# Constant products first on TensorE, the input check split, last outputs in two passes and a new order for the first four graphs, in a two-layer graph transformer

## The chip, the cores and the metric

The kernel runs on one core of a Trainium2 chip. The metric is the device time of one execution in microseconds (us), the median of several runs. A core has engines that run side by side, each with its own queue of instructions that it works off in order: PE (TensorE, matrix products; PEld is the loading of their weights), DVE (VectorE), ACT (ScalarE), POOL (GpSimd) and SP (SyncE, which only issues transfers here). Engines wait for one another through semaphores.

## The reference, cut to what matters

64 graphs of 256 nodes with 256 features, all float32, go through two attention layers of 8 heads of 32. Layer 0 weighs values by the relation that stands in `adj` (0 or 1 in these inputs) and has a feed-forward part of 1024; layer 1 masks by `adj` and normalises a joined product.

```python
# layer 0
q, k = heads(src @ Wq + bq), heads(src @ Wk + bk)
attn = softmax(q @ k.T / sqrt(32))
out = sum((attn * (adj == r)) @ heads(src @ Wv[r] + bv[r]) for r in range(4))
x = ln(src + out @ Wo + bo, g1, beta1)
x = ln(x + gelu(x @ W1 + b1) @ W2 + b2, g2, beta2)
# layer 1
e = heads(x @ Wq) @ heads(x @ Wk).T
e = where(e >= 0, e, 0.2 * e)
h = softmax(where(adj > 0, e, -9e15)) @ heads(x @ Wv)
out = ln(h, g1, b1)
out = ln(concatenate([out, x]) @ Wffn.T, g2, b2) + x
```

## The kernel before, in words

One graph is one program of some 140 steps (`program`, in `fast_path`). A step is an emit function with an engine and the tiles that it reads and writes; a helper like `linear_T`, `score`, `stats` or `normalise` appends it, so many rows of the profile bear the line of a helper. A graph's names end in digits: `q0` and `k0` are the transposed queries and keys of layer 0, `q1` and `k1` those of layer 1.

The steps of all 64 graphs are merged into one list by `in_order` (line 46): each step has a key, `g * PERIOD` plus an offset, and the list is sorted by it. For the middle graphs the offset comes from `STARTS`, for the first four from `FIRST`, for the last three from `LAST`; keys are no times, only the order counts. Every engine gets its own steps in the order of the list. At the ends (`at_end`: the first two graphs, the last three) a matrix is transposed by products with `ident` on PE (line 413); in between it goes through DRAM (lines 387 to 400).

Per graph on PE: `pq0`, `pk0` (line 351), `pva0` and `pva1` (values, line 668, which need `wv0` with the difference of its two relations, line 600 on DVE), two groups of scores `s` (line 487), weighted sums `po` (lines 526 and 533), `pwo`, the feed-forward products `ph` and `pw2` (lines 716 and 734), then layer 1. Around them ACT takes exponentials (line 503) and adds biases from `cols` (line 375; its first such step also loads a table), DVE adds the mask to scores (line 512), takes reciprocals (line 542) and statistics (lines 453 to 457), and POOL makes `neg` from `adj` (line 646), adds pairs (line 559) and raises variances to -0.5 (`rs`, line 462, 128x2).

All loads are issued by SP: those of the weights by `fetch` (line 571), those of a graph by `load` (line 342). Their order at the start is `xT`, `cols`, `wk0`, `wq0`, `x`, `wf`, `wv0` (two), `rows` (the first three), `adj`, `wk1`, `wq1`, `wo`, the next `xT`, `w2`, the rest of `rows`, `w1`. Eight transfers can be out: a later one waits for the landing of the one eight places ahead.

Some constants are prepared on the way, by steps of graph 0: `bf` is a product of `wide` and `wf` (line 613, copied at 618), `wf` is scaled by a gain (line 620), and `pmean` (line 624) is a product of `mean_w` with it, which line 630 subtracts. Lines 604 and 605 add shifts in `rows`.

The fast path holds for inputs within limits. Every graph leaves 13 `flags` per partition: sums of exponentials from ACT (line 503), a count of `adj` (`junk`, line 650) and minima of `po` from DVE (line 550). At the end of the program lines 823 to 830 compare all 64 x 13 of them, take the minimum into `held`, add that up over the partitions by a product (`pheld`, line 829) and turn it into an integer, `bad`. Every engine loads `bad` into a register (line 1106) and branches over a general path that isn't run with these inputs (line 1107).

A graph's output is `(pwa - mean) * rs3 * g21 + x2`: `normalise` (line 468), a product with the row `g21` (line 479), a sum (line 811), and a store by SP (line 815). The last two graphs (`alone`) do all three on DVE, the others the last two on POOL.

Of the kernel before, what the change touches and what calls it, by code (L numbers as in the profile page):

```python
# [20 lines left out]
LIMIT = 1.0e30  # L21
# [13 lines left out]
class Op:  # L35


    __slots__ = ("eng", "name", "emit", "reads", "writes", "tiles", "g")

    def __init__(self, eng, name, emit, reads, writes, g):  # L40
        self.eng, self.name, self.emit, self.g = eng, name, emit, g
        self.reads, self.writes = reads, writes
        self.tiles = {k.partition("/")[0] for k in (*reads, *writes) if not k.startswith("c_")}


def in_order(programs, starts, period, first, last):
# [4 lines left out]
    for g, p in enumerate(programs):  # L51
# [75 lines left out]
        -10256.79, -10417.946, -10418.845, -9655.276, -9647.458, -9418.15, -8780.756, -8806.383, -9016.741, -9513.158,  # L127
        -9495.078, -8590.155, -10003.295, -9291.904, -8309.175, -9386.676, -9231.17, -8787.021, -8660.76, -8501.398,
        -10584.811, -10218.322, -9608.334, -9104.436, -8066.002, -8804.961, -9825.295, -9578.272, -9914.488, -9442.87,
        -8813.641, -8607.962, -8849.406, -8632.071, -8937.919, -8812.934, -8791.331, -8734.75, -8483.473, -8864.473,  # L130
        -8822.078, -8429.134, -8776.728, -8405.192, -7953.761, -7894.531, -8299.242, -8717.176, -8646.31, -8662.099,
        -8343.426, -8329.008, -8597.096, -8514.051, -8426.417, -8189.977, -7960.378, -7718.59, -7712.398, -7156.11,
        -7563.49, -7208.499, -7179.238, -6917.369, -6917.367, -6842.704, -6710.303, -6711.003, -5706.559, -6495.228,
        -6280.588, -5865.4, -5592.334, -6199.311, -5863.221, -6468.444, -6370.931, -4538.172, -4524.407, -4477.482,
        -4262.426, -3973.372, -3910.404, -3900.969, -3877.771, -3834.718, -3824.557, -3691.587, -3679.897, -3639.541,
        -3597.827, -3679.895, -3670.439, -3501.055, -3451.404, -3588.256, -3531.636, -2474.703, -2461.465, -2676.921,
        -2656.758, -3125.063, -3042.896, -2882.815, -2732.056, -2363.914, -1353.064, -2880.589, -2907.254, -2822.537,
        -2673.746, -2335.009, -1303.618, -1270.494, -1110.428, -1102.74, -2879.234, -2657.203, -2352.556, -2279.244,
        -2160.732, -1901.876, -2634.306, -2653.396, -2012.309, -2009.408, -1888.68, -1502.012, -1412.116, -1401.834,
        -1416.364, -1030.225, -1028.517, -845.649, -962.518, -780.505, -766.279, -749.221, -709.195, -670.931,  # L140
        -611.671, -592.943,
    ],
    [
        -9082.793, -8821.413, -8584.273, -7679.799, -6811.314, -7104.159, -8654.94, -8159.713, -8706.211, -7742.971,
        -7680.585, -6931.674, -7419.902, -7096.988, -7703.279, -7671.026, -7657.377, -6498.021, -7183.946, -7456.855,
        -7450.09, -7209.053, -7018.734, -5702.193, -5336.158, -5268.731, -5511.652, -7298.293, -6672.664, -6484.273,
        -6263.457, -6347.867, -6896.885, -6809.914, -6006.901, -5819.284, -5608.438, -5269.483, -4803.162, -5294.853,
        -4599.474, -4599.472, -4523.688, -4264.846, -4180.662, -4093.925, -3856.605, -3530.581, -2717.744, -3767.55,
        -3761.457, -3803.533, -3754.922, -3678.334, -3632.2, -3255.184, -2820.341, -2245.675, -2226.134, -2052.422,
        -2039.8, -1660.362, -1625.035, -1571.564, -1553.578, -1513.777, -1477.183, -1431.984, -1430.337, -1422.225,  # L150
        -1283.864, -806.335, -713.143, -1134.104, -964.675, -1040.209, -962.322, -637.997, -270.909, -429.146,
        -415.015, -902.241, -790.878, -678.22, -644.005, -304.133, -210.429, -750.975, -854.699, -673.468, -515.045,
        -207.195, 203.932, 204.235, 208.581, 204.66, -655.094, -463.233, -624.339, -356.78, -220.376, 151.773,
        -324.271, -584.5, -91.29, 187.862, 205.121, 208.965, 211.757, 217.346, 216.045, 221.82, 233.633, 247.638,
        251.141, 252.624, 253.253, 254.651, 255.687, 261.447, 266.334, 284.16,
    ],
    [
        -4966.772, -5312.443, -5889.946, -5039.664, -5159.898, -4403.862, -4858.218, -4629.529, -4776.965, -4743.102,
        -3624.438, -3257.491, -3668.955, -3429.095, -4199.202, -3902.433, -4134.244, -3680.958, -3569.518, -4163.448,
        -3791.904, -3660.555, -3903.418, -3088.911, -2951.813, -2855.197, -2965.02, -3779.594, -3631.033, -3662.701,  # L160
        -3261.638, -3534.707, -3599.126, -3348.893, -3327.559, -3335.702, -3058.321, -2879.469, -2723.157, -2940.722,
        -2500.765, -2419.982, -2276.826, -2220.814, -2013.151, -1889.428, -1759.468, -1742.956, -1603.331, -1264.512,
        -1189.663, -1485.202, -1299.287, -1432.334, -1367.98, -1493.639, -1413.183, -1010.364, -835.846, -342.676,
        -201.659, -201.446, -56.663, 32.587, 88.02, 119.909, 119.911, 119.913, 128.596, 142.281, 150.543, 153.74,
        168.786, 168.788, 169.449, 224.646, 270.798, 169.527, 175.654, 169.451, 170.984, 176.522, 181.529, 216.866,
        216.884, 176.871, 180.112, 181.424, 192.101, 195.643, 195.645, 177.642, 178.723, 179.252, 183.741, 199.835,
        208.317, 210.029, 210.062, 209.5, 181.49, 189.03, 182.007, 192.546, 208.878, 210.609, 189.653, 192.363,
        200.391, 206.241, 210.864, 218.9, 223.499, 223.501, 220.829, 224.953, 229.115, 229.117, 239.344, 239.346,
        237.172, 242.289, 242.553, 242.555, 246.814, 255.425, 276.721, 301.931,
    ],  # L170
    [
        -2616.915, -3738.122, -3620.23, -2516.76, -1581.888, -1074.953, -2411.766, -2359.837, -2551.424, -1876.812,
        -1291.539, -1214.653, -2577.138, -2502.882, -1561.046, -1537.605, -1435.037, -1321.017, -1285.438, -1542.519,
        -1499.312, -1171.673, -1282.107, -975.95, -721.667, -614.834, -791.494, -1342.782, -1251.881, -1324.781,
        -1047.049, -1006.905, -1196.205, -1109.182, -970.883, -1012.21, -901.837, -576.093, -575.311, -594.413,
        -511.897, -399.597, -363.529, -361.357, -259.089, -121.886, 103.011, 105.823, 105.825, 129.412, 150.16,
        113.575, 113.766, 138.118, 144.328, 134.023, 139.222, 135.909, 142.051, 154.14, 154.142, 155.882, 156.568,
        157.309, 157.311, 157.661, 157.915, 158.185, 158.711, 159.186, 159.188, 160.249, 160.251, 160.956, 167.451,
        210.29, 232.587, 171.569, 175.025, 170.655, 175.703, 199.606, 201.092, 184.548, 190.236, 177.141, 177.143,
        178.154, 178.156, 184.769, 199.293, 178.1, 178.056, 178.58, 195.805, 196.124, 204.141, 205.044, 205.046,  # L180
        205.281, 183.277, 193.889, 188.544, 197.528, 200.755, 203.056, 190.546, 183.279, 190.548, 190.55, 204.236,
        208.318, 210.997, 213.457, 212.603, 216.36, 216.673, 219.934, 223.927, 223.929, 220.362, 224.498, 225.099,
        229.925, 229.927, 233.872, 233.874, 233.876,
# [39 lines left out]
        9503.563, 10042.577, 10382.53, 9566.925, 10478.524, 10510.355, 10670.284, 10757.907, 10767.9, 11156.775,  # L223
        11402.842,
# [12 lines left out]
        16007.55, 16095.484, 16016.502, 16372.924, 17323.706, 17389.259, 17464.619, 17489.423, 17525.145, 17585.795,  # L237
# [4 lines left out]
def fast_path(nc, tc, a, out, bad):  # L242
# [13 lines left out]
    with ExitStack() as ctx:  # L256
# [64 lines left out]
        def program(g):  # L321
# [7 lines left out]
            def op(eng, reads, writes, emit):  # L329


                for w in writes:
                    name, _, tag = w.partition(":")
                    tags.setdefault(name, tag or name)
                writes = [w.partition(":")[0] for w in writes]
                name = writes[0] if writes else f"{eng}:{reads[0]}"
                used[name] = used.get(name, 0) + 1
                o = Op(eng, f"{name}#{used[name]}" if used[name] > 1 else name, emit, reads, writes, g)
                ops.append(o)
# [225 lines left out]

            if g == 0:

                def fetch(name, *pairs):
                    def emit():
                        for t, ap in pairs:  # L570
                            nc.sync.dma_start(out=t, in_=ap)
# [566 lines left out]
```

## Time and profile before

| what | us |
|---|---|
| median of 3 runs (2815.0 to 2818.29) | 2815.79 |
| the profiled execution | 2813.84 |
| its span, first to last instruction | 2812.1 |
| PE busy | 2779.5 |
| DVE, POOL, ACT busy | 2071.8, 1988.2, 1939.3 |
| mean granted TensorE clock | 0.998 of full |

In the profile a row of the timeline has its start and its length in us, engine, line, operation, the tile written and those read, shapes, and in brackets how long the engine was idle before it and what ended that. A product of float32 shows as two records. The table of stages has, for each stretch, its length, then for each engine its busy time and number of instructions (PE, PEld, DVE, ACT, POOL), the granted TensorE clock, the share of the transfer engines and GB/s. Rows with q behind the engine's name are its queue: issues, register loads, branches and waits; there the columns are the number, then least, median and greatest length in ns, then first and last start. Lines of the profile are those of the kernel before, unless said otherwise.

### The profile page before, as it was taken

To read this page: it belongs to the slowest core of one execution; us is meant where nothing else is said; L and a number is where in the kernel's file an instruction comes from. 1 tells how busy PE (TensorE), PEld (TensorE's weight loads), DVE (VectorE), ACT (ScalarE), POOL (GpSimd) and SP (SyncE) were. 2 spreads that over 40 slices of the span, in tenths; PEclk is the share of its full clock that TensorE was granted. 3 is DMA by queue.
4 is the path that set the end of the run, shared out by engine and by line. 5 is a ranking of instruction groups with operands and counts; after the bars stand their busy time and mean duration, and the time that the engine had idled before them with its cause. 6 is when DMAs were issued, how large, how long until landed. Compare 5 with 4: busy or idle time off the path is not lost.

```text
span 2812.1 us, 54239 instructions
## 1 busy us (share of the span) xinstructions
PE 2779.5 (99%) x21094; PEld 2085.7 (74%) x21094; DVE 2071.8 (74%) x3853; ACT 1939.3 (69%) x3131; POOL 1988.2 (71%) x1526
## 2 busy tenths in 40 slices
PE   8999999999999999999999999999999999999996
PEld 6777777777777777777777777777777777777774
DVE  5667777777777777777777777777777777777776
ACT  5766767767767667677676676776766767767663
POOL 3668677677676676776766867768667677677773
PEclk9999999999999999999999999999999999999999
DMA  3012122222222222222222222222222122231100
GB/s 132 24 46 71 52 75 61 54 72 57 61 65 58 68 61 54 73 59 58 69 61 61 62 52 76 57 57 69 60 61 64 51 74 60 54 83 49 50 27 13
DMA packets 269750, 169.55 MB, mean 60 GB/s; under 512 B 18608, under 2 KB 268976, under 8 KB 269488
## 3 DMA queue, kind: packets, MB, share of 16 engines
q1 hardware_dynamic: 269488, 166.02, 22.2%
q8 instruction: 169, 2.77, 0.4%
q14 instruction: 93, 0.76, 0.1%
HBM read 102.77 MB, written 63.18 MB: 59 GB/s over the span
## 4 chain that ended last, share of the span: by engine, by line
PE 93%; DVE 3%; POOL 1%; ACT 1%; DMA 1%; issue 1%; SPq 0%; DVEq 0%; POOLq 0%; ACTq 0%
PE pw L734 15%; PE ph L716 15%; PE po L526 12%; PE s L487 9%; PE pk L351 8%; PE pva L668 8%; PE pq L351 7%; PE pv L365 4%; PE pwo L365 4%; PE po L533 4%; PE pwb L365 4%; PE pwa L365 4%; DVE rd L542 1%; POOL e L768 1%; DVE e L512 0%
## 5 line engine op out<-in xcount | busy, mean ns | idle before, releaser
L559 POOL TENSOR_TENSOR es<-e 128x512 f32<-128x512 f32 x504 | 636.8, 1275 | 582.9 <-issue 455.8
L768 POOL TENSOR_TENSOR e<-e,m 128x1024 f32<-128x1024 f32 x252 | 595.2, 2374 | 103.1 <-DVE e L512 95.1
L716 PE MATMUL ph<-y0T,w 128*128 128x256 f32 x2048 | 464.8, 380 | 1.3 <-ACT y0T L432 0.9
L542 DVE RECIPROCAL rd<-po 128x256 f32<-128x256 f32 x256 | 440.3, 1737 | 33.5 <-PE po L533 33.3
L734 PE MATMUL pw<-w,hT 128*128 128x256 f32 x2048 | 452.9, 379 | 0.0
L503 ACT ACTIVATE e<-e 128x1024 f32<-128x1024 f32 x256 | 268.6, 1050 | 263.4 <-POOL e L768 262.5
L716 PEld LDWEIGHTS ph<-y0T,w 128*128 128x128 f32 x2048 | 388.0, 190 | 82.0 <-issue 16.2
L734 PEld LDWEIGHTS pw<-w,hT 128*128 128x128 f32 x2048 | 389.0, 190 | 53.2 <-issue 0.4
L512 DVE TENSOR_TENSOR m<-s,neg 128x1024 f32<-128x1024 f32 x256 | 310.9, 1217 | 107.3 <-ACT e L503 80.2
L503 ACT ACTIVATE e<-s 128x1024 f32<-128x1024 f32 x256 | 261.1, 1023 | 173.9 <-DVE m L512 89.7
L512 DVE TENSOR_TENSOR e<-s,neg 128x1024 f32<-128x1024 f32 x256 | 305.1, 1213 | 15.1 <-PE s L487 12.7
L764 ACT ACTIVATE m<-s 128x1024 f32<-128x1024 f32 x252 | 252.2, 1026 | 66.7 <-PE s L487 41.2
L487 PE MATMUL s<-q,k 32*128 32x256 f32 x4096 | 294.3, 400 | 2.1 <-ACT q L564 1.3
L487 PEld LDWEIGHTS s<-q,k 32*128 32x128 f32 x4096 | 185.5, 184 | 128.7 <-issue 51.3
L526 PE MATMUL po<-e,v 128*32 128x256 f32 x4096 | 271.7, 382 | 3.9 <-ACT v L564 3.0
L503 ACT ACTIVATE m<-m 128x1024 f32<-128x1024 f32 x256 | 265.4, 1070 | 4.1 <-DVE m L512 4.0
L668 PE MATMUL pva<-wv,xT 128*128 128x512 f32 x512 | 246.4, 604 | 0.0
L462 POOL TENSOR_TENSOR rs<-ve,neg_half 128x2 f32<-128x2 f32 x256 | 179.8, 702 | 88.0 <-DVE ve L457 83.6
L503 ACT ACT_TABLE_LOAD x127 | 162.9, 1283 | 90.3 <-PE s L487 89.1
L723 ACT ACTIVATE hT<-ph,cols 128x256 f32<-128x256 f32 x512 | 208.8, 476 | 11.5 <-PE ph L716 9.8
L676 DVE TENSOR_TENSOR v<-pva,rows 128x512 f32<-128x512 f32 x128 | 87.3, 683 | 169.2 <-PE pva L668 169.1
L526 PEld LDWEIGHTS po<-e,v 128*32 128x32 f32 x4096 | 119.8, 109 | 113.3 <-issue 41.0
(101 smaller groups left out, 4646.3 us busy)
## 6 DMA issues: line engine op xcount, KB each, us to landing
xT<-xT_dram SPq DMA_DIRECT2D x64, 256.0 KB, 3.3
x<-x_dram SPq DMA_DIRECT2D x64, 256.0 KB, 3.0
adj<-adjT_dram SPq DMA_DIRECT2D x64, 256.0 KB, 3.7
out_dram<-y SPq DMA_DIRECT2D x64, 256.0 KB, 2.2
y0d<-y0b SPq DMA_DIRECT2D x236, 64.0 KB, 1.8
y0r<-y0d SPq DMA_DIRECT2D x59, 256.0 KB, 2.8
y1d<-y1b SPq DMA_DIRECT2D x236, 64.0 KB, 1.8
y1r<-y1d SPq DMA_DIRECT2D x59, 256.0 KB, 2.8
```

Of the source, the lines that this page charges most:

```text
L351: nc.tensor.matmul(pt[:, o, :], lhsT=w[:, c, o * P : (o + 1) * P], rhs=s[:, c, :], start=(c == 0), stop=(c == KC - 1),)
L365: nc.tensor.matmul(pt[:, t, :], lhsT=T(s)[:, c, t * P : (t + 1) * P], rhs=w, start=(n == 0), stop=(n == len(parts) - 1),)
L487: nc.tensor.matmul(s[j // 2][:, j % 2, c, :], lhsT=kT[r, hg, c * P : (c + 1) * P], rhs=qT[r, hg, :], start=True, stop=True,)
L503: nc.scalar.activation(T(dst)[:, j], s, AF.Exp, scale=scale, **kw)
L512: lambda: nc.vector.tensor_tensor(T(dst)[:, j], T(src), T("neg")[:, None].to_broadcast([P, 2, NT, D]), ALU.add),
L526: nc.tensor.matmul(po[j * DH : (j + 1) * DH, 0, :], lhsT=v(c, j), rhs=T(e)[:, j, c, :], start=(n == 0 and c == 0), stop=(n == len(parts) - ...
L542: op("DVE", [po], [f"{rd}:rd"], lambda: nc.vector.reciprocal(T(rd), T(po)[:, 1, :]))
L559: lambda: on.tensor_tensor(T(dst)[:, j], T(e)[:, j, 0, :], T(e)[:, j, 1, :], ALU.add),
L668: nc.tensor.matmul(pv.rearrange("p r d -> p (r d)"), lhsT=s[:, c, t * P : (t + 1) * P], rhs=wv0[:, c].rearrange("p r d -> p (r d)"), start ...
L716: nc.tensor.matmul(ph[:, i, :], lhsT=w1[:, c, (f + i) * P : (f + i + 1) * P], rhs=s[:, c, :], start=(c == 0), stop=(c == KC - 1),)
L734: nc.tensor.matmul(T("pw2")[:, t, :], lhsT=T("hT")[:, f + i, t * P : (t + 1) * P], rhs=w2[:, f + i, :], start=(f + i == 0), stop=(f + i == ...
L768: nc.gpsimd.tensor_tensor(T(f"e1{hg}")[:, j], T(f"e1{hg}")[:, j], T(f"m1{hg}")[:, j], ALU.add)
```

## The change

- PE gets nine products of two constants, `ones` and `mean_w`, as its first instructions. Nobody reads them.
- `wk0` is issued by ACT's queue instead of SP's. The order of SP's loads is new: `wq0`, `xT`, `wf`, `cols`, `rows` (the first three), `wv0` (two), `x`, `adj`, `wv1`, `wq1`, `wk1`, the next `xT`, the rest of `rows`, `x`, `w1`, `wo`, `w2`.
- `FIRST` is written anew, so the first four graphs are ordered otherwise. In that order: `pq0` stands before `pk0`; `bf`, the scaling of `wf` and `pmean` stand before graph 0's first masked scores on DVE and before its second scores on PE; on DVE lines 604 and 605 stand before graph 0's second masked scores; on ACT the count of graph 1's `adj` stands one exponential further ahead of `y0T`. From some 220 us of the old profile on, every engine's order is that of before. `LAST` loses one key in each of the last two graphs.
- The flags of the first 63 graphs are compared as soon as the last of them is written (`check_most`), on DVE between `flags` and the z step of graph 62. Those of the last graph are compared after its own last flag (`check_last`), and `pheld` follows at once: in PE's queue it stands before the transposes of graph 63's `o1`.
- `bad` is converted after step `rs3` of graph 63, and every engine loads it there (`values_load`); on DVE that stands between the last `ve` and the output's passes, on SP before the last store. The branch stays at the end.
- For the last two graphs the output is made in two passes on DVE: `(pwa - mean) * g21`, which doesn't need `rs3`, then `* rs3 + x2`.

```diff
-                def fetch(name, *pairs):
+                def fetch(name, *pairs, queue="SP"):
                     def emit():
                         for t, ap in pairs:
-                            nc.sync.dma_start(out=t, in_=ap)
-
-                    op("SP", [], [f"c_{name}"], emit)
+                            (nc.sync if queue == "SP" else nc.scalar).dma_start(out=t, in_=ap)
+
+                    op(queue, [], [f"c_{name}"], emit)
+
...
                 fetch("wq0", (wq0, chunked(a["L0_gnn_Wq"])))
-                fetch("wk0", (wk0, chunked(a["L0_gnn_Wk"])))
+                fetch("wk0", (wk0, chunked(a["L0_gnn_Wk"])), queue="ACT")
                 fetch("cols", (cols, a["cols"]))
...
 
             op("DVE", ["pwa", "rs2", "zb"], ["pwa"], emit_z)
             stats("pwa", 3)
-            normalise("pwa", 3, "y2")
-            rows_op("y2", "y2", g21, ALU.mult, ["c_rows1"], "DVE" if alone else "POOL")
-            eng = nc.vector if alone else nc.gpsimd
-            op(
-                "DVE" if alone else "POOL", ["y2", "x2"], ["y2"],
-                lambda: eng.tensor_tensor(T("y2"), T("y2"), T("x2"), ALU.add),
-            )
+            if alone:
+
+                def emit_centred_out():
+                    for t in range(NT):
+                        nc.vector.scalar_tensor_tensor(
+                            T("y2")[:, t, :], T("pwa")[:, t, :], T("mv3")[:, t, 0:1], g21, ALU.subtract, ALU.mult
+                        )
+
+                def emit_scaled_out():
+                    for t in range(NT):
+                        nc.vector.scalar_tensor_tensor(
+                            T("y2")[:, t, :], T("y2")[:, t, :], T("rs3")[:, t : t + 1], T("x2")[:, t, :],
+                            ALU.mult, ALU.add,
+                        )
+
+                op("DVE", ["pwa", "mv3", "c_rows1"], ["y2:y"], emit_centred_out)
+                op("DVE", ["y2", "rs3", "x2"], ["y2"], emit_scaled_out)
+            else:
+                normalise("pwa", 3, "y2")
+                rows_op("y2", "y2", g21, ALU.mult, ["c_rows1"])
+                op(
+                    "POOL", ["y2", "x2"], ["y2"],
+                    lambda: nc.gpsimd.tensor_tensor(T("y2"), T("y2"), T("x2"), ALU.add),
+                )
             op(
                 "SP", ["y2"], [],
                 lambda: nc.sync.dma_start(out=out[g].rearrange("(t p) d -> p t d", p=P), in_=T("y2")),
             )
             return ops
 
-        for o in in_order([program(g) for g in range(B)], STARTS, PERIOD, FIRST, LAST):
+
+        held = const.tile([P, FLAGS + 1], F32, name="held")
+        all_held = const.tile([P, 1], F32, name="all_held")
+
+        def compare(dst, src):
+            nc.vector.tensor_scalar(dst[:, :, :8], src[:, :, :8], LIMIT, None, ALU.is_lt)
+            nc.vector.tensor_scalar(dst[:, :, 8:9], src[:, :, 8:9], 0.25 * NT * D, None, ALU.is_equal)
+            nc.vector.tensor_scalar(dst[:, :, 9:], src[:, :, 9:], 1.0 / LIMIT, None, ALU.is_gt)
+
+        def check_most():
+            most = flags[:, : B - 1]
+            compare(most, most)
+            nc.vector.tensor_reduce(held[:, FLAGS:], most.rearrange("p b f -> p (b f)"), AX.X, ALU.min)
+
+        def check_last():
+            compare(held[:, None, :FLAGS], flags[:, B - 1 :])
+            nc.vector.tensor_reduce(all_held, held, AX.X, ALU.min)
+            pt = ps.tile([P, 2, D], F32, tag="g", bufs=4, name="pheld")
+            nc.tensor.matmul(pt[:1, 0, :1], lhsT=all_held, rhs=ones[:, :1], start=True, stop=True)
+            return pt
+
+
+        warm = ps.tile([P, 2, D], F32, tag="g", bufs=4, name="warm")
+        for _ in range(9):
+            nc.tensor.matmul(warm[:, 0, :P], lhsT=ones, rhs=mean_w, start=True, stop=True)
+
+        ops = in_order([program(g) for g in range(B)], STARTS, PERIOD, FIRST, LAST)
+        most = sum(o.flag for o in ops if o.g < B - 1)
+        rest = sum(o.flag for o in ops if o.g == B - 1)
+        failed = None
+        for o in ops:
             o.emit()
-
-
-        nc.vector.tensor_scalar(flags[:, :, :8], flags[:, :, :8], LIMIT, None, ALU.is_lt)
-        nc.vector.tensor_scalar(flags[:, :, 8:9], flags[:, :, 8:9], 0.25 * NT * D, None, ALU.is_equal)
-        nc.vector.tensor_scalar(flags[:, :, 9:], flags[:, :, 9:], 1.0 / LIMIT, None, ALU.is_gt)
-        held = const.tile([P, 1], F32, name="held")
-        nc.vector.tensor_reduce(held, flags.rearrange("p b f -> p (b f)"), AX.X, ALU.min)
-        pt = ps.tile([P, 2, D], F32, tag="g", bufs=4, name="pheld")
-        nc.tensor.matmul(pt[:1, 0, :1], lhsT=held, rhs=ones[:, :1], start=True, stop=True)
-        nc.vector.tensor_scalar(bad, pt[:1, 0, :1], -1.0, float(P), ALU.mult, ALU.add)
+            if o.flag and o.g < B - 1:
+                most -= 1
+                if most == 0:
+                    check_most()
+            elif o.flag:
+                rest -= 1
+            if o.flag and most == 0 and rest == 0:
+                verdict = check_last()
+            if o.g == B - 1 and o.name == "rs3":
+                assert most == 0 and rest == 0
+                nc.vector.tensor_scalar(bad, verdict[:1, 0, :1], -1.0, float(P), ALU.mult, ALU.add)
+                failed = nc.values_load(bad[0:1, 0:1])
+        return failed
 
 
 @with_exitstack
...
-        fast_path(nc, tc, a, out, bad)
-        failed = nc.values_load(bad[0:1, 0:1])
+        failed = fast_path(nc, tc, a, out, bad)
         with tc.If(failed > 0):
             general_path(nc, tc, a, out)
```

## The prediction

> **What bounds the kernel now.** I read the page first, then busy time by stage, the timeline of the first 40 us, the timeline of the last 20 us, and the two lines of code that end the kernel.
>
> ```profile
> PE 2779.5 (99%) x21094; PEld 2085.7 (74%) x21094; DVE 2071.8 (74%) x3853; ACT 1939.3 (69%) x3131; POOL 1988.2 (71%) x1526
> ```
>
> TensorE is busy 2779.5 of 2812.1 us, so only 32.6 us are not products. Where they lie, by stage (after the stretch: its length, then PE's busy time, then the others'):
>
> ```profile
> 0.00:10.00 10.00, 4.76 (x12) 3.91 (x13) 0.81 (x6) 1.28 (x1) 0.69 (x6) 1.00 0.74 222
> 30.00:40.00 10.00, 8.43 (x45) 5.31 (x44) 8.74 (x18) 6.65 (x14) 6.34 (x6) 1.00 0.31 96
> 160.00:200.00 40.00, 39.36 (x286) 30.45 (x286) 26.12 (x53) 27.10 (x45) 29.59 (x23) 1.00 0.09 21
> 200.00:250.00 50.00, 49.47 (x382) 36.36 (x382) 37.58 (x67) 33.77 (x54) 32.53 (x25) 1.00 0.27 69
> 2800.00:2813.00 13.00, 0.19 (x2) 0.11 (x2) 5.19 (x15) 0.00 (x0) 0.69 (x1) 0.56 0.08 25
> ```
>
> The head leaves PE idle for 5.24 us, then 0.64 (10 to 20 us), 1.57 (30 to 40), 0.12, 0.64 and 0.53; from 250 to 2650 us nothing at all; the rest, 23.8 us, lies behind 2650 us, 11.9 of it behind 2800 us. Only the first five or so graphs get another order and only the last chain gets other instructions. In between the order is word for word the same, and PE is full: the middle moves in time and keeps its length.
>
> ```profile
> 5.24 3.75 PE L351 MATMUL pk<-xT,wk 128*128 128x256 f32 x8 [5.24 <-DMA wk<-L_gnn_Wk_dram]
> 8.79 2.27 PE L351 MATMUL pq<-xT,wq 128*128 128x256 f32 x8
> ...
> 12.55 0.69 DVE L600 TENSOR_TENSOR wv<-wv 128x512 f32<-128x512 f32 x1 [8.20 <-DMA wv<-L_gnn_Wv_dram]
> ...
> 13.42 3.70 PE L668 MATMUL pva<-wv,xT 128*128 128x512 f32 x8
> ...
> 14.21 0.62 POOL L646 TENSOR_SCALAR neg<-adj 128x512 f32<-128x512 int32 x1 [12.91 <-DMA wo<-L_gnn_Wo_dram]
> ...
> 18.86 1.13 PE L624 MATMUL pmean<-wf,mean_w 128*128 128x256 f32 x4 [0.45 <-DVE wf L620]
> ...
> 37.86 7.20 PE L716 MATMUL ph<-y0T,w 128*128 128x256 f32 x32 [0.87 <-ACT y0T L432]
> ```
>
> Two limits overlap here. The first eight products take 3.75 us and the same form later 1.89: TensorE starts at half speed. But `pva` starts when VectorE has taken the difference of `wv`, which lands at 12.55, and `neg` starts when `adj` lands at 14.2. The transfers are nearly full from 3 to 25 us and come in the order in which they were issued.
>
> ```profile
> 2796.07 0.41 DVE L550 TENSOR_REDUCE flags<-po 128x1 f32<-128x256 f32 x1
> 2796.20 0.55 PE L413 MATMUL po<-ident,o 128*128 128x128 f32 x3 [1.92 <-DVE o L545]
> ...
> 2801.80 0.99 DVE L468 TENSOR_SCALAR y<-pwa,mv,rs 128x256 f32<-128x256 f32 x2 [0.81 <-POOL rs L462]
> ...
> 2804.27 0.37 SPq L815 DMA_DIRECT2D out_dram<-y  x1
> ...
> 2806.33 0.15 DVE L830 TENSOR_SCALAR bad<-pheld 1x1 int32<-1x1 f32 x1 [0.37 <-PE pheld L829]
> ```
>
> ```profile
> L1106 DVEq TENSOR_LOAD <-bad x1: 539/539/539, 2806.5 to 2806.5; - x1
> ...
> L1107 PEldq COMPARE_BRANCH  x1: 3909/3909/3909, 2807.1 to 2807.1; - x1
> ...
> L1134 SPq EVENT_SEMAPHORE  x10: 17/28/2942, 2807.8 to 2812.0; - x10
> ```
>
> The last output is issued at 2804.27 and lands 2.1 us later, at 2806.4. The kernel ends 5.7 us after that: the check runs behind the output, every engine loads its verdict, PE's branch over the general path takes 3.91 us, and SP's 2.94 us wait is for PE.
>
> **The change, part by part.**
>
> *Nine constant products at the front.* They need `ones` and `mean_w`, ready at 1.1. Cold, a record of 256 columns took 3.75/8 = 0.47 us, so one of 128 takes about 0.235; nine products of two records are 4.2 us, 1.1 to 5.3. The first real product had its data at 5.24, so they cost at most 0.1 to 0.6 us there. The Trainium skill (TensorE: Matmul & The Clock Gate, "What's actually happening") has the array at half clock until it has been busy for some 3.4 us; by that rule both first products run at 1.89 and the change wins 3.75 + 2.27 - 2 x 1.89 = 2.2 us. The row of `pva` says otherwise: what stands behind those products waits for `wv` until 13.4. I book nothing; the ends are 0 and -2.2. That the clock falls back in the wait for `wv` I exclude: 3.0 us of idle at 2786 left the next products at their usual length.
>
> *`wk0` through ACT's queue, other order of the loads.* Bytes up to and with `wv`: before 2060 KB, now 2188 (rows overtake x); 256 KB more took 0.74 us late in this queue, so +0.4, and `wv` is issued 0.5 us earlier. On the second queue the same skill (DMA: Bandwidth & Descriptors, "Issuing engines are not separate DMA queues") says that it saves the issuing time alone; one issue here took 0.43 to 0.51 us. So `wv` lands at 12.6 and `pva` starts at 13.5 instead of 13.42. `adj` stands behind 2700 KB both times: 14.2 again, and with it `neg` and the masked scores at 14.87. `cols` now stands behind `wf`: before, `wf` with 1548 KB was in at 11.0 (the SP queue's wait for it); with 1280 KB, reckoned from 2.6, about 9.6, so `cols` at 9.9 instead of 3.83. ACT needs then 1.28 (table) + 0.84 + 0.84 to give q and k, and the scores start at 12.9 instead of 12.35. They take 1.08 and end at about 14.0, so `pva` can slip to 13.5 to 14.0. Price 0.1 to 0.6; taken 0.3.
>
> *`bf`, the scaled `wf` and `pmean` ahead of the masked scores.* They now fill VectorE's wait for `neg`. From 17.05 to 23.37 PE ran scores 1.35, a wait of 0.45, then pmean, pk, pq; now 0.97 + 1.08 + 2 x 1.73 = 5.5 instead of 6.3: -0.8. VectorE's two shifts stand ahead of the second masked scores and need `rows1`, which should land at 19.4 (4620 KB; it was 22.3 behind 5644): near enough to hide; if it is a us late, this -0.8 is gone.
>
> *`adj`'s count ahead of `y0T` on ACT.* In front of `ph`, ACT ran junk (0.71 + 0.19) before `y0T`; it now comes one step earlier, in a wait for scores. `ph` waited 0.87 for it: between 0 and -0.9, taken -0.5. So `ph` starts 0.3 later, 0.8 and 0.5 earlier: -1.0.
>
> *The rest of the four orders.* Two waits are left in PE, 0.64 at 162 us and 0.53 at 209 us, both for ACT's copies of q and k. The new order can take away at most 1.2; it can also bring as much. ACT and DVE are two thirds busy there. Taken -1.0. **Head: -2.0** (from +0.5 to -4.2).
>
> *Check of the first 63 graphs inside graph 62's chain.* Four instructions on VectorE, by their old rows 2804.16 to 2805.96: 1.8 us, between `flags` (2774.8) and the z step (2775.62). 0.8 of it fills a wait for `pwa`; 1.0 pushes. *Two passes for graph 62:* before: wait for POOL 0.8, 0.99 + 0.72 + 0.72; now two passes of 1.02 (the row of L799, the same form, twice), the first under POOL's step: -1.1. The next masked scores start at 2781.0 as before: nothing.
>
> *Last check in graph 63.* Three small compares, 0.12 apart like `ve`'s, a minimum over 14 (0.17), the hand-over (0.14 from `held` to `pheld`), `pheld` 0.19. In PE's queue `pheld` stands before the transposes of `o`, and those release the statistics: all behind them is late. Transposes started at 2796.20; now 2796.48 + 0.36 + 0.17 + 0.14 + 0.19 = 2797.3: +1.1.
>
> *Verdict converted and loaded behind the last statistics, two passes.* From `ve` (2801.0) to the output's issue were 3.27 us. Now VectorE converts (0.15), loads (0.54, with hand-overs 0.8, beside POOL's 0.70) and does two passes of 1.02: 2.9. -0.4. The output is issued at 2804.27 + 1.1 - 0.4 = 2805.0 and lands at 2807.1. PE loads at 2802.2 and branches until 2806.7, before that landing; if PE's branch were not hidden, it would cost what it passes 2807.1. Behind the landing stand SP's waits, 2807.2 to 2808.2 before, some done ahead of it, and 0.9 to the end: 2808.4 to 2809.0, taken 2808.7 instead of 2812.1. **Tail: -3.4** (from -2.6 to -4.0).
>
> Sum: 2812.1 - 2.0 - 3.4 = 2806.7 of span; the profiled execution had 1.7 us around its span (2813.84), and the median of 3 stands 2.0 above that execution. Against the median: 2815.8 - 5.4 = 2810.4.
>
> **Rivals.**
>
> *The warm start pays in full.* For it: transfers ran at 222 GB/s in the first 10 us and at 367 in the next 10, so earlier or denser issue could bring `wv` and `adj` sooner, and then the 2.2 us come out. Against it: the bytes ahead are as many. 2808.2.
>
> *The head gives nothing.* The new orders trade one wait for another, as PE and DVE wait for each other by turns until 38 us (DVE is busy 8.74 of 10). Only the tail is left: 2812.4.
>
> *Slower: `cols` behind `wf`.* All of graph 0 hangs on q and k, these on `cols`, 2.96 us of ACT before the first scores. Landing after 10.5 it costs its delay one for one: the gain is gone at 15.9, 0.2% is lost at 21.5. If it comes with the weights queued behind it, at 22: 2821.9. Against it: 12 KB, fourth in its queue.
>
> **Numbers.** A measurement tells 0.2% (5.6 us) from no change here, so 2810.2 is the line. The forecast, 0.57, at 2810.4, is spread by 1.5 and half of it lies on each side; full warm start 0.25, faster; empty head 0.13, same; `cols` 0.05, slower. Faster 0.53, same 0.42, slower 0.05. The range takes in the forecast's bounds and most of the first two rivals: 2807.8 to 2812.8.
>
> **What would show it.** `pk` and `pq` at 1.9 us each, yet `pva` at 13.3 to 14.0; `pmean` without a wait; `ph` near 36.9; from 250 us on every row about 2 us earlier; `pheld` ahead of the transposes and those 1.1 us later after `o`; the output's landing, and no longer PE's branch, before the last waits. Wrong if `wv` lands before 12 or `cols` after 10.5, or if SP's last waits still end on PE.

## The result and the profile after

The changed kernel took 2810.3 us (median of 13 runs, 2808.51 to 2811.49) against 2818.29 for the kernel before in the same session (13 runs, 2812.4 to 2819.43): a ratio of 0.9977, with a 95% interval of 0.9969 to 0.9986. The predicted time was 2810.4. That these two agree to 0.1 is luck: the forecast was 5.4 less than a median of 2815.8, and measured side by side the kernels differ by 8.0. One execution of the kernel before, in a later session, took 4471.71 us at a mean granted clock of 0.603; it is left out of every figure below. The profiled execution took 2811.49 with a span of 2809.7, only 2.4 less than the profiled execution of before, so that pair shows less than the medians do; why is the main question below. First the page's line of the engines:

```profile
PE 2785.5 (99%) x21112; PEld 2090.4 (74%) x21112; DVE 2070.7 (74%) x3857; ACT 1939.3 (69%) x3131; POOL 1988.5 (71%) x1526
```

TensorE is busy 6.0 us longer than before: 4.2 are the constant products, and what `pq` and `pk` save is outweighed by later products that ran at half speed. The stages, in the columns of before:

```profile
0.00:10.00 10.00, 8.82 (x38) 7.91 (x38) 0.80 (x6) 2.61 (x5) 0.69 (x6) 1.00 0.80 247
30.00:40.00 10.00, 8.59 (x39) 5.51 (x38) 7.65 (x15) 9.52 (x17) 8.31 (x8) 0.83 0.26 80
160.00:200.00 40.00, 40.00 (x290) 30.53 (x288) 27.33 (x55) 26.08 (x44) 28.73 (x22) 1.00 0.08 22
200.00:250.00 50.00, 50.00 (x388) 37.43 (x388) 38.70 (x68) 35.38 (x57) 32.73 (x26) 1.00 0.25 69
2800.00:2813.00 13.00, 0.74 (x2) 0.01 (x1) 3.87 (x13) 0.00 (x0) 0.69 (x1) 0.68 0.08 25
```

The waits at 162 and 209 us are gone: TensorE is full from 40 to 2650 us. But from 30 to 40 us the granted clock is 0.83 where it was 1.00. (In the first microseconds the column says 1.00 only because the trace's record of the clock starts with its first rise to full, at 9.54 us before and at 5.98 after; over all profiles it rises at 5.2 to 7.0 us with the products at the front and at 8.5 to 10.8 without them.) The timeline of the head (start, length, work, and in brackets the wait before it):

```profile
1.18 4.21 PE L861 MATMUL warm<-mean_w,ones 128*128 128x128 f32 x18 [1.18 <-DVE half L297]
5.29 2.30 PE L350 MATMUL pq<-xT,wq 128*128 128x256 f32 x8
...
10.89 0.69 DVE L600 TENSOR_TENSOR wv<-wv 128x512 f32<-128x512 f32 x1 [3.00 <-DMA wv<-L_gnn_Wv_dram]
...
11.69 3.67 PE L669 MATMUL pva<-wv,xT 128*128 128x512 f32 x8 [0.44 <-PE s L485]
...
12.48 0.77 POOL L646 TENSOR_SCALAR neg<-adj 128x512 f32<-128x512 int32 x1 [11.19 <-DMA adj<-adjT_dram]
...
15.20 1.03 PE L624 MATMUL pmean<-wf,mean_w 128*128 128x256 f32 x4
...
35.88 8.89 PE L717 MATMUL ph<-y0T,w 128*128 128x256 f32 x32 [0.66 <-ACT y0T L431]
```

`wv` and `adj` are in 1.7 us earlier than in the profile of before, `pva` starts 1.73 earlier and `ph` 1.98 earlier. Then the 32 products of `ph` take 8.89 us instead of 7.20, and what is left at 300 us is 1.59. The tail:

```profile
2796.01 0.41 DVE L548 TENSOR_REDUCE flags<-po 128x1 f32<-128x256 f32 x1
...
2796.98 0.19 PE L855 MATMUL pheld<-ones,all_held 128*1 128x1 f32 x2 [3.72 <-DVE all_held L853]
2797.10 0.66 PE L412 MATMUL po<-ident,o 128*128 128x128 f32 x4
2797.59 3.14 PE L364 MATMUL pwa<-wf,o 128*128 128x256 f32 x8
...
2800.85 1.02 DVE L800 SCALAR_TENSOR_TENSOR pwa<-pwa,rs,zb 128x256 f32<-128x256 f32 x2 [1.89 <-PE pwa L364]
...
2803.79 0.88 DVE L811 SCALAR_TENSOR_TENSOR y<-pwa,mv,rows 128x256 f32<-128x256 f32 x2 [0.66 <-DVE bad L879]
2804.59 0.87 DVE L817 SCALAR_TENSOR_TENSOR y<-y,rs,x 128x256 f32<-128x256 f32 x2
2805.48 0.37 SPq L833 DMA_DIRECT2D out_dram<-y  x1
```

`pheld` stands ahead of the transposes, as predicted. But `pwa` takes 3.14 us instead of 1.89, and the z step (L800), which used to wait for POOL's statistics, now waits for `pwa`. The queues at the branch over the general path:

```profile
L1157 SPq EVENT_SEMAPHORE  x8: 17/17/17, 2806.1 to 2808.3; - x8
...
L1157 PEldq COMPARE_BRANCH  x1: 3970/3970/3970, 2803.8 to 2803.8; - x1
...
L1157 PEldq EVENT_SEMAPHORE  x1: 51/51/51, 2807.8 to 2807.8; - x1
```

PE's branch still takes 3.97 us, but it begins before the output is issued and ends at 2807.7; the output lands at 2807.9 and SP's last waits follow that. From the issue to the end are 4.2 us where there were 7.8.

### The profile page after: what moved, and what is told of

It reads as the page before. It is cut to its first block, busy times and chain, and to the rows that moved or that the text cites. A ratio compares the mean times of both kernels' runs of the same rounds, so it can differ in the third digit from the quotient of the medians.

```text
span 2809.7 us, 54277 instructions
## 1 busy us (share of the span) xinstructions
PE 2785.5 (99%) x21112; PEld 2090.4 (74%) x21112; DVE 2070.7 (74%) x3857; ACT 1939.3 (69%) x3131; POOL 1988.5 (71%) x1526
## 4 chain that ended last, share of the span: by engine, by line
PE 97%; DVE 2%; ACT 0%; POOL 0%; issue 0%; DMA 0%; SPq 0%; DVEq 0%; POOLq 0%; ACTq 0%
PE ph L717 16%; PE pw L735 16%; PE po L524 12%; PE s L485 10%; PE pk L350 8%; PE pva L669 8%; PE pq L350 8%; PE pv L364 4%; PE po L531 4%; PE pwo L364 4%; PE pwa L364 4%; PE pwb L364 4%; DVE rd L540 1%; ACT e L501 0%; DVE e L510 0%
```

## The experiments

Sessions differ in the kernel before: its medians were 2815.74 (2812.63 to 2819.17), 2816.61 (2812.11 to 2818.94) and 2815.03 (2812.51 to 2819.47). Its lowest times agree and its medians don't, so differences are read within a session; across sessions anything below 1 us is not read.

| session, kernel | median (lowest to highest), runs | ratio to before, 95% |
|---|---|---|
| 1 no products at the front | 2812.42 (2808.44 to 2813.87), 21 | 0.9985, 0.9979 to 0.9992 |
| 1 before with the products alone | 2814.21 (2811.78 to 2818.18), 13 | 0.9995, 0.9986 to 1.0003 |
| 1 tail alone | 2812.59 (2809.09 to 2816.78), 21 | 0.9989, 0.9983 to 0.9996 |
| 1 `wk0` on SP | 2811.07 (2808.54 to 2814.24), 21 | 0.9983, 0.9977 to 0.9990 |
| 2 changed kernel again | 2810.13 (2807.76 to 2812.25), 12 | 0.9981, 0.9972 to 0.9990 |
| 2 changed, waits filled | 2807.66 (2807.37 to 2807.97), 7 | 0.9969, 0.9957 to 0.9980 |
| 2 changed, `pheld` late | 2808.59 (2806.84 to 2809.46), 8 | 0.9972, 0.9961 to 0.9982 |
| 2 changed, filled and late | 2806.89 (2806.28 to 2807.15), 6 | 0.9969, 0.9956 to 0.9981 |
| 3 before, waits filled | 2813.67 (2812.97 to 2814.33), 13 | 0.9994, 0.9986 to 1.0002 |
| 3 tail alone, filled | 2810.46 (2809.36 to 2811.17), 18 | 0.9980, 0.9973 to 0.9988 |
| 3 changed without products, filled | 2809.24 (2808.21 to 2809.64), 11 | 0.9979, 0.9970 to 0.9988 |
| 3 changed, filled, again | 2808.36 (2807.45 to 2808.93), 10 | 0.9975, 0.9965 to 0.9984 |

**What releases `pva`.** My theory was the prediction's (the loads, so the products at the front are worth nothing); the rival was that the first products, at half speed, stand in the way. Two kernels with the products taken away and put in alone:

```diff
-        warm = ps.tile([P, 2, D], F32, tag="g", bufs=4, name="warm")
-        for _ in range(9):
-            nc.tensor.matmul(warm[:, 0, :P], lhsT=ones, rhs=mean_w, start=True, stop=True)
```

> The changed kernel without the nine constant products; all else is as in it. Theory of the prediction (the products are worth 0, the loads set the start of pva): pva stays at 11.7 us, within 0.3, and the time within 0.5 us of the changed kernel's. Rival (with the loads 1.7 us earlier, the first products at half speed stand in the way): pq and pk take 2.3 and 3.7 us instead of 2.3 and 1.9, the first scores end near 12 to 13 instead of 11.2, pva starts at 12.5 to 13.3, and every row from 250 us on is 1 to 1.7 us later than in the changed kernel: about +1.5 us. If the products also keep TensorE at full clock later on, up to +3.

The timeline of this kernel:

```profile
5.16 3.75 PE L350 MATMUL pq<-xT,wq 128*128 128x256 f32 x8 [5.16 <-DMA xT<-xT_dram]
8.71 2.93 PE L350 MATMUL pk<-xT,wk 128*128 128x256 f32 x8
...
11.01 0.69 DVE L600 TENSOR_TENSOR wv<-wv 128x512 f32<-128x512 f32 x1 [2.64 <-DMA wv<-L_gnn_Wv_dram]
11.68 0.84 ACT L374 ACTIVATE k<-pk,cols 128x256 f32<-128x256 f32 x2 [1.68 <-PE pk L350]
12.43 1.15 PE L485 MATMUL s<-q,k 32*128 32x256 f32 x16
13.51 1.55 PE L669 MATMUL pva<-wv,xT 128*128 128x512 f32 x3
```

`wv` is ready at 11.7 and `pva` starts at 13.51, at the end of the scores, which waited for `k`, which waited for `pk`. The rival's rows came, a little later even than it said: `ph` at 37.13 instead of 35.8. The theory of the prediction fell. (In this timeline and the next two the last row is cut off near 14.5 us; `pva` is 3.7 us long in all three.) The median, 2812.42, gives no clean price: the changed kernel wasn't in that session, and `ph` ran at half speed in this profile. The price is taken from the filled pair below.

> The kernel before plus the nine constant products at TensorE's front, and nothing else. Theory of the prediction: pk and pq take less (about 1.9 each instead of 3.75 and 2.27), pva still waits for wv until about 13.4, and the time is that of before within 0.5 us. Rival (the warm start pays in full): pva and all behind it 1.5 to 2.2 us earlier.

The same three lines were added to the kernel before. `pva` started at 12.10 and `ph` at 36.51, 1.3 us earlier than in the profile of before, and all rows to 2547 us stayed 1.4 earlier. The time, 0.9995 of before, can't be told from no change: in the profiled execution `pwa` of graph 62 took 3.08 us instead of 1.89, after which nothing of the gain was left (graph 63's first scores at 2779.98 instead of 2779.63).

> The changed kernel with the first four graphs ordered as before, all first loads on SP in the old order and no constant products: only the early check, the early verdict and the two passes of the output remain of the change. Prediction: -3.4 us against before (from -2.6 to -4.0), with the output issued 1.1 - 0.4 = 0.7 later than before and the end 4.2 us after that issue instead of 7.8. Theory that the tail carries the whole change: -8, the difference of the two medians. Theory that the head carries most of it: about -1, as in the profiled pair, where the last products run at half speed and cost 1.2.

Edit: `FIRST`, the order of the loads and their queue as before, no products at the front. Its head is thus that of before, word for word, and its timeline shows what one profile of before had hidden:

```profile
10.79 0.69 DVE L600 TENSOR_TENSOR wv<-wv 128x512 f32<-128x512 f32 x1 [6.34 <-DMA wv<-L_gnn_Wv_dram]
...
11.99 0.84 ACT L374 ACTIVATE k<-pk,cols 128x256 f32<-128x256 f32 x2
12.52 1.15 PE L485 MATMUL s<-q,k 32*128 32x256 f32 x16 [0.43 <-ACT k L374]
13.60 1.13 PE L669 MATMUL pva<-wv,xT 128*128 128x512 f32 x2
```

`wv` is in 1.7 us earlier than in the profile of before, with the same order of loads on the same queue; `pva` is not. In the profile of before, `wv`'s difference ended at 13.24 and the scores at 13.42: two limits fell together, and I named one of them. On time the tail alone gave 3.2 us (2815.74 to 2812.59).

**The second queue.**

```diff
-                fetch("wk0", (wk0, chunked(a["L0_gnn_Wk"])), queue="ACT")
+                fetch("wk0", (wk0, chunked(a["L0_gnn_Wk"])))
```

> The changed kernel with the load of wk0 issued by SP, second in its queue behind wq0, instead of by ACT's queue. If the order of the loads brought wv and adj in 1.7 us earlier (rows and wf early, x behind wv): wv lands at 10.8 to 11.3 and adj at 12.4 to 12.9, and the time stays within 0.5 us. If the second queue did it: wv near 12.5, adj near 14.1, pva near 13.4, and the time 1.5 to 2 us above that of the changed kernel.

```profile
6.52 1.97 PE L350 MATMUL pq<-xT,wq 128*128 128x256 f32 x8 [1.13 <-DMA xT<-xT_dram]
...
11.80 0.69 DVE L600 TENSOR_TENSOR wv<-wv 128x512 f32<-128x512 f32 x1 [3.03 <-DMA wv<-L_gnn_Wv_dram]
12.59 2.38 PE L669 MATMUL pva<-wv,xT 128*128 128x512 f32 x5 [0.45 <-PE s L485]
```

`xT` landed at 6.4 instead of 5.0 to 5.2, though `wk0` landed ahead of it both ways, at 4.2 to 4.4. The row of `wv` is 0.9 later than in the profile of the changed kernel, between the two expectations, and 0.3 to 1.3 later than in the eight profiles with `wk0` on ACT's queue (10.53 to 11.47). `ph` came 0.7 to 0.8 later than in the two profiles of the changed kernel; the time, 2811.07, is too near the 2810.1 to 2810.3 of the changed kernel in other sessions to be told apart.

**The clock.** In the changed kernel's profile three groups of products took longer than in the profile of before, with a granted clock below 1. Is it the change, or chance? The changed kernel was run again:

> The changed kernel once more, to stand beside the next three on one chip. Times of 2808.5 to 2813, median about 2810.5. Theory of the clock: the profile shows half-speed products after one or more of four waits (ph at 36 us, graph 62's transposes at 2771, po of graph 63 at 2788, pwa at 2798), and which of them are slow differs from the profile of the changed kernel taken before. Rival (each wait always leads to the same clock): ph at 8.9 us, po and pwa slow as there, the transposes' products not.

Granted clock in three stretches (third column from the right), first of the profile of the changed kernel, then of this second one:

```profile
36.00:40.00 4.00, 4.00 (x11) 3.09 (x12) 2.18 (x2) 3.97 (x7) 3.92 (x5) 0.59 0.37 125
2770.00:2774.00 4.00, 2.66 (x15) 2.24 (x16) 3.96 (x15) 1.02 (x2) 1.95 (x3) 1.00 0.00 0
2786.00:2794.00 8.00, 5.22 (x64) 2.43 (x64) 3.46 (x5) 4.19 (x9) 3.27 (x1) 0.79 0.01 2
```

```profile
36.00:40.00 4.00, 4.00 (x19) 3.41 (x19) 2.08 (x2) 3.97 (x7) 3.92 (x4) 1.00 0.34 115
2770.00:2774.00 4.00, 3.92 (x13) 3.40 (x14) 3.42 (x13) 1.02 (x2) 3.29 (x3) 0.58 0.00 0
2786.00:2794.00 8.00, 6.17 (x60) 2.87 (x64) 3.22 (x4) 3.98 (x9) 3.08 (x1) 0.57 0.01 2
```

The same program: `ph` slow in the one, graph 62 slow in the other. So the program alone doesn't decide where the clock falls. All profiles without filled waits, each group's length in us (full speed: 7.20, 1.89, 1.07, 1.89):

| profile | `ph` after waits of 0.58 to 0.66 and 0.65 to 0.87 | `pwa` of graph 62, after 2.08 | first `po` of graph 63, after 2.99 | `pwa` of graph 63, after 1.7 to 3.7 |
|---|---|---|---|---|
| before | 7.20 | 1.89 | 1.07 | 1.89 |
| before with the products | 7.20 | 3.08 | 1.07 | 1.89 |
| tail alone | 7.20 | 1.89 | 1.07 | 1.89 |
| changed | 8.89 | 1.90 | 1.94 | 3.14 |
| changed, again | 7.20 | 3.09 | 1.93 | 2.90 |
| no products at the front | 8.88 | 1.90 | 1.93 | 3.38 |
| `wk0` on SP | 7.20 | 2.96 | 1.93 | 2.87 |
| `pheld` late | 7.20 | 3.17 | 1.82 | 1.89 |

In this table the first `po` of graph 63 looks like a matter of the order: slow in all five profiles of the new one, in none of the three of the old. The trace's record of the clock shows what decides. In all profiles the clock changes only at moments that are multiples of 3.41 us apart, and where this grid lies against the program's start differs from execution to execution. Two stretches of the grid around that wait of 2.99 us, first of the changed kernel, then of the kernel before:

```profile
2784.43:2787.84 3.41, 0.62 (x3) 0.19 (x2) 2.63 (x3) 2.62 (x6) 2.69 (x2) 1.00 0.00 0
2787.84:2791.25 3.41, 3.21 (x32) 1.59 (x36) 0.00 (x0) 2.35 (x5) 1.44 (x1) 0.50 0.02 5
```

```profile
2784.58:2787.99 3.41, 1.90 (x8) 1.34 (x8) 3.41 (x4) 2.25 (x4) 2.69 (x2) 1.00 0.01 2
2787.99:2791.40 3.41, 1.93 (x34) 1.17 (x36) 0.51 (x1) 3.12 (x6) 2.74 (x1) 1.00 0.00 0
```

In the first the wait falls into one stretch, of which TensorE is busy for 18%; in the second the grid halves it, and TensorE is busy for 56 and 57%. In the eight profiles every stretch at full clock in which TensorE was busy for at most 39% was followed by half speed, and none in which it was busy for more than 62%. In between busy time doesn't decide alone: one of nine from 42 to 57% was followed by it, and two of eleven from 58 to 62%, both with `ph` behind them. What else counts there is open, and with five profiles against three the split by order may be chance.

To test whether filled waits hold the clock, products of constants (the fillers) were put into them, into the tile that the next product overwrites:

```diff
+        def keep_busy(tile, n):
+            for _ in range(n):
+                nc.tensor.matmul(tile[:, 0, :P], lhsT=ones, rhs=mean_w, start=True, stop=True)
+
+        FILL = {(0, "py0"): 2, (0, "ph0"): 2, (B - 2, "po1"): 8, (B - 1, "po10"): 12}
...
+            if (o.g, o.name) in FILL:
+                keep_busy(at_(o.g, o.name), FILL[o.g, o.name])
             o.emit()
...
+            keep_busy(pt, 14)
             nc.tensor.matmul(pt[:1, 0, :1], lhsT=all_held, rhs=ones[:, :1], start=True, stop=True)
```

> The changed kernel with products of constants put into TensorE's waits: two before the first transposes of graph 0 (y0), two before its first ph, eight before graph 62's transposes of o1, twelve before graph 63's first po of layer 1, fourteen before pheld; all written into the tile that the next product overwrites. Theory of the clock (the waits make TensorE fall to half speed, by chance): ph 7.2 us, po of graph 63 and pwa at full speed (pwa 1.9 us), granted clock 1.00 in every stage but the first and last, times close together near the lowest of the changed kernel, 2808 to 2809: about -2.5 on the median. Rival (the spread comes from elsewhere, the loads for one): the spread of 3 to 5 us stays and the median moves by less than 1.

```profile
36.00:40.00 4.00, 4.00 (x23) 3.59 (x22) 1.82 (x2) 3.97 (x7) 3.92 (x4) 1.00 0.26 89
2770.00:2774.00 4.00, 3.64 (x20) 3.26 (x20) 3.97 (x14) 1.02 (x2) 3.30 (x3) 1.00 0.00 0
2786.00:2794.00 8.00, 7.54 (x94) 5.22 (x93) 5.25 (x10) 2.69 (x6) 1.80 (x1) 1.00 0.00 0
```

Full clock in every stretch, times within 0.6 us instead of 4.5, and the median 2.5 lower: as the theory of the clock had it. In the new order `ph0` is not the first of the `ph` steps, so the two fillers named for it ran between products, filled nothing and cost 0.45; those ahead of the transposes of `y0` were enough: TensorE is busy for 77% of the stretch of the grid ahead of `ph` instead of 58 to 62%.

> The kernel before with products of constants in TensorE's waits at the same places as in the two kernels with fillers (two before graph 0's first transposes of y0, two before its first ph, eight before graph 62's transposes of o1, twelve before graph 63's first po of layer 1, eleven before its transposes). Theory of the clock: the spread of the kernel before, 2812 to 2819, comes from stretches at half speed behind these waits, so the times close up at 2811 to 2812.5, 4 to 5 us below its median. Rival (its spread comes from the two waits at 162 and 209 us, which the change removes and which are not filled here): single times up to 3.4 us higher remain.

The kernel before, filled likewise (eleven products ahead of graph 63's transposes), closed up from a spread of 7 us to 1.4. So its spread was the clock's too, and the waits at 162 and 209, not filled here, don't carry it. The level was 1.2 us above the upper end of what I had written: the fillers push the transposes by 0.2, the branch took 0.26 longer than in the profile of before, and the rest is not settled.

**The price of each part at full clock.** Three more, with the same fillers.

> The kernel with the tail of the change alone (old order, old loads, no products at the front), with the fillers, fourteen of them before pheld. Against the kernel before with fillers it gives the price of the tail at full clock: -3.4 by the prediction, less the part of the transposes that pheld pushes (already in it). If the tail's gain was in truth a gain of clock, it is less than 2.

> The changed kernel with the fillers, without the nine products at the front. Against the one with both it gives the price of the warm start: 0 by the prediction; +1.3 to +1.4 by the rows of the two traces (ph at 37.13 instead of 35.78), if the first scores, and not wv, release pva.

> The changed kernel with the fillers once more, as the common end of the three differences: 2807.4 to 2808.0. Against the tail alone with fillers it gives the price of the head: -2.0 by the prediction, -2.8 by the rows at 300 us of the traces whose ph ran at full speed (303.96 and 301.19); against the kernel before with fillers the whole change at full clock: -5.4 by the prediction, about -4 if the kernel before closes up at 2811.5.

From the medians of that session: the whole change 2813.67 to 2808.36, -5.3; its tail 2813.67 to 2810.46, -3.2; its head 2810.46 to 2808.36, -2.1 (-2.5 without the 0.45 that the fillers inside `ph` cost in the new order alone); of the head, the products at the front 2809.24 to 2808.36, -0.9. The fillers cost the kernel before 0.2 and the tail alone 0.1 (`rd` to z), and the longer branch of the former counts too, so these differences are good to about 0.3 us.

**`pheld` ahead of the transposes.**

```diff
             compare(held[:, None, :FLAGS], flags[:, B - 1 :])
             nc.vector.tensor_reduce(all_held, held, AX.X, ALU.min)
+
+        def add_up():
             pt = ps.tile([P, 2, D], F32, tag="g", bufs=4, name="pheld")
...
-                verdict = check_last()
+                check_last()
+            if o.g == B - 1 and o.name == "pwa":
+                verdict = add_up()
```

> The changed kernel with the product pheld issued behind graph 63's last product pwa instead of ahead of its transposes of o1; the compares stay where they are. Prediction (pheld ahead of the transposes costs 1.1): the transposes start 0.75 to 0.9 after the row of flags ends less than now, at the end of o as in the kernel before, z starts 0.9 to 1.1 earlier, and the time is about 1 us less. Rival (pheld is hidden): no change within 0.3.

```profile
2796.12 0.55 PE L412 MATMUL po<-ident,o 128*128 128x128 f32 x3 [1.73 <-DVE o L543]
2796.50 1.89 PE L364 MATMUL pwa<-wf,o 128*128 128x256 f32 x8
2798.33 0.19 PE L857 MATMUL pheld<-ones,all_held 128*1 128x1 f32 x2
2798.70 1.02 DVE L800 SCALAR_TENSOR_TENSOR pwa<-pwa,rs,zb 128x256 f32<-128x256 f32 x2 [0.81 <-POOL rs L461]
```

Beside the changed kernel, whose last `rd` (the reciprocal ahead of graph 63's `o`) starts within 0.03 us of this one's, the transposes are 1.0 earlier and z 2.15 earlier. Of that, 1.0 is `pheld`'s place and the rest is `pwa` at full speed, behind a wait of 1.73 instead of 3.72.

> Both: pheld behind pwa, and the fillers (eleven before graph 63's transposes instead of the fourteen before pheld). If both theories hold, the effects add: about -3.5 on the median of the changed kernel, near 2807, with all times within some 1.5 us. If the fillers stand in the way of the products that they precede, the transposes start later than in the kernel with pheld late alone, by what the fillers overrun.

It gave 2806.89, 0.8 below the filled kernel and 3.2 below the changed one, where 3.5 was expected. The effects don't add in full: alone the fillers gave 2.5 and the late `pheld` 1.5, and in its one profile the late `pheld` too left `pwa` at full speed. The fillers do stand in the way a little: `rd` to z is 5.06 us here and 4.84 in the unfilled kernel with `pheld` late. With `pheld` early it is 6.00 filled and 5.90 unfilled (tail alone), so `pheld` costs 0.94 to 1.06. This version is faster than both kernels.

## Why the prediction was right, and where it was not

The sum, -5.4, holds: -5.3 at full clock. The tail was right by its mechanism. The head's sum was right by luck: three of its terms were wrong and one too large, and they offset each other. The clock was missing altogether.

- **The warm start, booked at nothing: wrong.** It is worth 0.9 us by the times and 0.8 to 1.35 by the row of `ph`. The step that failed is "The row of `pva` says otherwise: what stands behind those products waits for `wv` until 13.4". It waited for the scores as much, and these for `pk` and `pq` at half speed. The rule of the Trainium skill that I set against the row (TensorE: Matmul & The Clock Gate, "What's actually happening") gave 2.2 and was the better guide; not all 2.2 came, because then `wv`, ready at 11.2 to 12.2, is the next limit (`pva` 11.6 to 12.3).
- **The loads, +0.3 with `wv` at 12.6 and `adj` at 14.2: wrong, and not the change's doing.** `wv` landed at 10.80; the prediction's own sign "Wrong if `wv` lands before 12" came true. With the old order it landed at 10.4 to 11.0 as well in four other profiles; the 12.46 of the profile of before was the latest of all profiles, since `wf` alone took 3.9 us there. A rate reckoned from one profile was carried over to another execution. The `cols` rival didn't come: they landed at 7.31, and `k` had to wait for `pk` until 9.3 anyway.
- **`pmean` ahead, -0.8: wrong.** `pmean` had no wait, as written, but the second scores then took 1.82 instead of 1.35: they need the space of the first ones, which ACT reads later (the trace has them wait 0.39 for its exponential). The rows that VectorE's two shifts need were in by 17.6, so they are not the reason. From the start of `pva` to graph 0's first `po` are 9.87 us after and 9.95 before. In the other profiles it is 9.6 to 9.9 in the new order with the products at the front and 9.3 without them, 9.3 in three of the old order and 9.9 in one, which has the products. So the old order reaches 9.3 too, and nothing like 0.8 came of the reordering.
- **`adj`'s count, -0.5: oversized.** The two waits before `ph` were 0.58 and 0.87 and are 0.64 and 0.66: -0.15.
- **The two later waits, -1.0: right.** Both are gone in all profiles of the new order; they were 0.64 and 0.35 to 0.53. So the head's -2.0 stands against -2.1 measured, with the warm start in the place of the reordering on DVE and ACT, which the forecast had at nothing and its first rival in full.
- **The early check and graph 62, nothing: right.** From graph 62's transposes to graph 63's first scores are 9.82 us in both profiles.
- **`pheld`, +1.1: right.** 0.94 to 1.06 by `rd` to z, 0.8 by the times.
- **Verdict and two passes, -0.4: right in kind, too small.** From z to the output's issue were 5.50 us and are 4.63, -0.87: the passes took 0.88 and 0.87, not twice 1.02.
- **The end behind the landing: right.** 4.2 us after the issue (4.0 to 4.3 filled), 3.7 predicted, with the branch ending 0.2 ahead of the landing. These 0.5 too many and the 0.5 of the line above cancel. The tail's -3.4 stands against -3.2.
- **What was missing: the clock.** "That the clock falls back in the wait for `wv` I exclude: 3.0 us of idle at 2786 left the next products at their usual length." At the wait for `wv` nothing fell, but the reason doesn't hold: after that same wait of 2.99 us `po` ran at half speed in all five profiles of the new order that were not filled; in the profile of before, where it kept its speed, the grid of 3.41 us halves the wait. One observation of a wait that leaves the clock up excludes nothing. That the changed kernel's profile shows only 2.4 us of the gain is this: about 1.7 were lost in `ph`, 1.4 in `po` and 1.0 in `pwa`. That adds up to 6.5, more than 5.3; the head of the profile of before was also the slowest of its order (`ph` at 37.86; 36.84 to 37.42 in the three others without the products).

The unfilled medians differ by 6.5 to 8.0 in two sessions, more than 5.3. The remainder is the clock in the kernel before. Each execution's mean granted clock is on record: in the third session 21 executions of before at 0.998 took 2812.51 to 2815.66, five at 0.997 took 2815.03 to 2815.84, and 15 at 0.996 took 2817.49 to 2819.47; 0.002 of 2813 us are 5.6. The changed kernel has such executions too, but its spread is 4.5 us instead of 7. No profile of a long execution of before was taken, so which places it loses in is open.

## What to carry to other kernels

Where a row waits for one thing, look for what else became ready within a few tenths at that moment, since taking one limit away then pays nothing or everything; a second profile of the same kernel tells which of them moves. Short waits of TensorE can cost more than their length, because the products behind them may run at half speed: a few products of constants into a tile that is about to be overwritten hold the clock, if they are shorter than the wait and really stand in it. A product that only carries a verdict belongs behind the last real product, not in front of the chain that ends the kernel.

## What the runs showed of the hardware

- The clock fell behind waits of 2.08 us in four of eight profiles, behind two waits of 0.64 and 0.66 within 2.3 us in two of five, and behind 2.99 us in five of eight. Once down it stayed down for 3.41 us or twice that, and its changes lie on a grid of 3.41 us. The Trainium skill (TensorE: Matmul & The Clock Gate, "What's actually happening") speaks of an idle window of about 3.4 us that runs freely. The free-running window agrees with the traces; that it must be idle does not: the clock fell behind stretches of the grid in which TensorE was busy for up to 44% of the time, and twice ahead of `ph` for 58%.
- One load moved to a second queue brought the next ones in earlier by more than its issue: `xT` at 5.0 to 5.2 instead of 6.4, where one issue takes 0.43 to 0.48. The same skill (DMA: Bandwidth & Descriptors, "Issuing engines are not separate DMA queues") has the issuing time alone saved. One profile stands against eight, so this is a hint.
- Landing times of the same loads in the same order differ between executions by up to 2.0 us (`wv` at 12.46 and 10.41).
